# Cross-attention for eight batches on one core: other signs in the seven-product form, and product 6 of y in blocks

## The chip, the core and the metric

One core of one Trainium2 chip. It has a matrix engine (TensorE, PE in the profile), three engines for elementwise work (VectorE, DVE; ScalarE, ACT; GpSimd, POOL), a queue engine that issues transfers (SyncE, SP), an on-chip memory, accumulation banks that PE writes (PSUM) and 16 DMA engines. Each engine runs its own list of instructions in the order in which it was written. The metric is the device time of one execution in microseconds, median of three runs.

## The reference

For each of 8 batches, with x1 and x2 of 512 x 1024 (channels c, positions n or m):

```
q = einsum('bcn,dc->bnd', x1, Wq) + bq          # d = 64
k = einsum('bcn,dc->bdn', x2, Wk) + bk
v = einsum('bcn,dc->bdn', x2, Wv) + bv
attn = softmax(einsum('bnd,bdm->bnm', q, k), axis=2)
out = einsum('bcm,bnm->bcn', v, attn) + x1
```

All of it is float32.

## The kernel before

**The arithmetic.** Per batch the kernel computes scores (m on partitions, n along the free axis), e = exp(score - max), then y = x2 times e, and out = Wv times (y / sum of e) + bv + x1. Both products, of y (stage "y") and of out (stage "o"), use the seven-product form of a 2 x 2 block multiplication. The left operand of y is x2 transposed in blocks a11 .. a22 with sums S1 .. S4, the right one is e in blocks t11 .. t22 (t11 and t21 for the first half of n, t12 and t22 for the second) with sums T1 .. T4. The products are numbered 1 to 7. Product 6 is S2 times T2, and its result is wanted together with product 1.

**Product in one piece or in blocks.** A product in one piece (`multiply`, L420) is 8 calls of the matrix multiply with 512 columns, which the trace shows as 16 instructions. A product in blocks (`multiply_seeded`, L595) is the same seven-product form once more inside: seven small products of two calls each with 256 columns, 28 instructions in the trace. For that DVE first makes inner sums of the left operand (`left_stream`, L478, four instructions) and of the right operand (`right_stream`, L491, three), and afterwards adds one small product to the result (`complete`, L626). ACT copies five partial results while PE works. Before, products 5, 7, 3 and 4 of y are done in blocks in all batches, 1 and 2 in batches 2 to 8, and product 6 in one piece (`first(6)`), added in PSUM on top of product 1.

**The order.** The order of every engine's work is written out by hand in `period` (L868), one call per batch; in the text "batch 1" is the one with s.b = 0. In the steady state PE runs, for batch s and the next batch n: y products 1, 2, 6; scores of n's first half and n's queries; y products 5, 7, 3; scores of n's second half and n's keys; y product 4; then o products 1, 6, 2, then 5, 7 and 3 mixed (`multiply_57`, L545), then o product 4, and batch n's product 1. `multiply_57` leaves o product 7 in bank c; DVE completes it (L591), reads it out with product 5's copy (`evict_o(s, "22")`, L716), and o product 4 (`second(4)`, L437 with output ps_oc) then accumulates on top in the same bank.

**The softmax.** The maximum over m of half h is taken by DVE over the tiles (`fold`, L248, L258) and by POOL across partitions (`highest`, L264); then DVE subtracts it tile by tile (`lower`, L299) and ACT takes the exponential (L308). The sum over m of the first half is made by transfers that add: ACT copies tile 0 (L729) and POOL issues three adding DMAs one after another (`add_tile`, L724), each adding to the same tile, so that each is issued when the one before has landed. The sum of the second half is made by DVE with three folds (L248, output "sum"). Both are then reduced across partitions by POOL (`total`, L269), sent to a column (`few`, L271), inverted by DVE (L277), sent to DRAM (`row`, L279) and spread back (L284).

**Sums made by transfers.** A DMA issued by POOL can add to its destination. S1 (from a block that SP loads), S2, S3, T3 and T4 (from a copy or a negated copy by ACT) are made in that way; S4 is a DVE instruction in batches 2 to 8 (L108). The results 11, 22 and 12 of out get x1 added in this way too (L720) before SP sends them out (L721).

In `period`, the place of the first half's third adding DMA and the second half's maximum:

```
        if five:
            weave(folds(n, 1, "max", ALU.max))
        complete_4 = multiply_seeded(s, 4, "r", hooks, "c" if n else "a")
        if five:
            highest(n, 1)
        complete_4()
        ...
        evict_y(s, "21")
        if five:
            add_tile(n, 0, 3)
            add_11(n, "S3")
        scale_y(s, "21")
```

## Time and profile before

| what | value |
|---|---|
| median of three runs (lowest, highest) | 678.31 us (677.18, 678.32) |
| the profiled execution: its time, its span | 677.15 us, 675.4 us |
| busy time of PE, DVE, ACT, POOL | 666.4, 612.5, 358.5, 218.2 us |
| moved by DMA | 134.26 MB, mean 199 GB/s |
| mean granted clock of PE | 0.998 |

A row of a timeline gives the start in microseconds, the duration, the engine, the line of the kernel, the operation, output and inputs, shapes and a count; in brackets stands idle time of the engine ahead of it and what ended that. Rows of one engine can overlap a little, because the duration runs to the write of the last result; the distance between two starts is what one instruction costs its engine. A matmul's end is modelled, so that PE too is read by distances between starts, and "the chain of waits in order of time" gives these as lengths. A window row gives each engine's busy time in a stretch with the number of instructions, the granted clock (PEclk), and the share of the DMA engines that was busy. The time of an execution is its span and 1.75 us around it (677.15 - 675.4).

### The profile page before, as it was taken

What the parts mean: (1) busy time and instruction counts of PE and PEld (TensorE: products, weight loads), DVE (VectorE), ACT (ScalarE), POOL (GpSimd) and SP (SyncE); (2) the same over time, 40 slices, a digit from 0 to 9 for tenths busy, and PEclk for the clock granted to TensorE, in tenths of its full rate; (3) what the DMA queues carried; (4) which work ended last, traced back from release to release, by engine and by line L of the source; (5) the groups of instructions that cost most, each with busy time, mean ns of one, the idle gap of its engine ahead of it and who ended that gap; (6) DMA issues with size and microseconds to landing.
All of it is one profiled execution on the core that took longest, in us unless ns stands there. A gap on an engine that the chain in (4) does not pass through costs nothing.

```text
span 675.4 us, 7565 instructions
## 1 busy us (share of the span) xinstructions
PE 666.4 (99%) x2510; PEld 413.1 (61%) x2510; DVE 612.5 (91%) x811; ACT 358.5 (53%) x619; POOL 218.2 (32%) x188
## 2 busy tenths in 40 slices
PE   8999999999999999999999999999999999999996
PEld 5334754766556665657656486574855757566853
DVE  1999999999999889998999979999899989999984
ACT  3755456366465464654745647445565456565321
POOL 0126206260344411642134411445122460153400
PEclk9999999999999999999999999999999999999999
DMA  9678798958997959969599695996969968489412
GB/s 304 272 207 278 190 264 152 247 116 245 249 212 192 196 172 301 173 184 249 152 276 190 179 267 151 240 214 175 270 108 222 218 136 231 94 154 251 80 42 98
DMA packets 51638, 134.26 MB, mean 199 GB/s; under 512 B 5648, under 2 KB 7952, under 8 KB 51600
## 3 DMA queue, kind: packets, MB, share of 16 engines
q0 software_dynamic: 23328, 57.75, 47.9%
q1 hardware_dynamic: 27984, 75.64, 31.0%
q10 hardware_dynamic: 288, 0.39, 0.2%
q8 instruction: 20, 0.33, 0.2%
q14 instruction: 18, 0.15, 0.1%
HBM read 88.35 MB, written 16.81 MB: 156 GB/s over the span
## 4 chain that ended last, share of the span: by engine, by line
PE 87%; DVE 7%; DMA 3%; POOL 1%; issue 1%; SPq 1%; ACT 0%; DVEq 0%; POOLq 0%
PE ps_yc L518 10%; PE ps_ya L437 7%; PE ps_oa L559 6%; PE ps_ya L518 5%; PE ps_oa L437 5%; PE ps_s L228 5%; PE ps_o L437 4%; PE ps_oc L437 4%; PE ps_o L457 4%; PE ps_q L181 4%; PE ps_k L181 3%; PE ps_i4chain L518 3%; PE ps_i5chain L518 3%; PE ps_i7chain L518 3%; PE ps_i3chain L518 3%; PE ps_i1chain L518 2%
## 5 line engine op out<-in xcount | busy, mean ns | idle before, releaser
L269 POOL PARTITION_ALL_REDUCE den<-sum x16 | 52.5, 3283 | 72.7 <-DVE few L277 52.6
L724 POOL DMA_DIRECT2D sum<-e x21 | 27.9, 1328 | 145.7 <-ACT sum L729 71.6
L299 DVE TENSOR_TENSOR e<-e,top 128x1024 f32<-128x1024 f32 x60 | 70.6, 1218 | 0.4 <-POOL top L264 0.4
L308 ACT ACTIVATE e<-e 128x1024 f32<-128x1024 f32 x60 | 61.5, 1055 | 8.4 <-DVE e L299 7.8
L237 ACT COPY e<-ps_s 128x1024 f32<-128x1024 f32 x46 | 45.7, 1031 | 8.3 <-PE ps_s L228 8.3
L437 PE MATMUL ps_ya<-eT,aS 128*128 128x512 f32 x112 | 49.5, 593 | 0.0
L228 PE MATMUL ps_s<-q,k 64*128 64x512 f32 x188 | 47.5, 609 | 0.8 <-ACT q L751 0.8
L264 POOL PARTITION_ALL_REDUCE top<-max x16 | 31.0, 1940 | 52.1 <-DVE few L277 20.4
L248 DVE TENSOR_TENSOR max<-max,e 128x1024 f32<-128x1024 f32 x30 | 36.7, 1225 | 2.5
L437 PEld LDWEIGHTS ps_ya<-eT,aS 128*128 128x128 f32 x112 | 21.2, 190 | 24.1 <-issue 23.5
L284 POOL DMA_DIRECT2D den<-row x16 | 9.0, 561 | 78.0 <-DMA row<-few 75.0
L228 PEld LDWEIGHTS ps_s<-q,k 64*128 64x128 f32 x188 | 16.8, 186 | 24.8 <-issue 16.3
L720 POOL DMA_DIRECT2D r<-in_x_dram x14 | 29.3, 2090 | 2.9 <-ACT r L711 2.9
L648 DVE TENSOR_TENSOR y<-y,den 128x1024 f32<-128x1024 f32 x24 | 29.3, 1220 | 0.2
L437 PE MATMUL ps_o<-y,w 128*128 128x512 f32 x64 | 28.8, 592 | 0.0
L457 PE MATMUL ps_o<-y,w 128*128 128x512 f32 x64 | 28.8, 592 | 0.0
L437 PE MATMUL ps_oa<-yT,w_S 128*128 128x512 f32 x64 | 28.8, 592 | 0.0
L437 PE MATMUL ps_oc<-yT,w 128*128 128x512 f32 x64 | 28.8, 592 | 0.0
L611 ACT COPY ps_yc<-ps_i7chain 128x256 f32<-128x256 f32 x32 | 11.4, 357 | 30.3 <-PE ps_i7chain L518 22.3
L611 ACT COPY ps_ya<-ps_i5chain 128x256 f32<-128x256 f32 x32 | 11.4, 358 | 29.9 <-PE ps_i5chain L518 25.7
L485 DVE TENSOR_TENSOR aI<-a,aI 128x256 f32<-128x256 f32 x60 | 26.0, 433 | 1.0
L611 ACT COPY ps_ya<-ps_i1chain 128x256 f32<-128x256 f32 x28 | 10.0, 357 | 30.6 <-PE ps_i1chain L518 27.0
(257 smaller groups left out, 1734.8 us busy)
## 6 DMA issues: line engine op xcount, KB each, us to landing
x_in_x_dram<-in_x_dram SPq DMA_DIRECT2D x60, 512.0 KB, 9.3
a<-in_x2T_dram SPq DMA_DIRECT2D x32, 512.0 KB, 9.5
sum<-e POOLq DMA_DIRECT2D x21, 512.0 KB, 7.5
eT<-eT POOLq DMA_DIRECT2D x16, 512.0 KB, 10.9
aS<-in_x2T_dram POOLq DMA_DIRECT2D x15, 512.0 KB, 7.4
uo<-in_x_dram POOLq DMA_DIRECT2D x14, 512.0 KB, 9.6
r<-in_x_dram POOLq DMA_DIRECT2D x14, 512.0 KB, 11.5
out_dram<-r SPq DMA_DIRECT2D x14, 512.0 KB, 3.4
```

The lines of the kernel that those rows point to most:

```text
L181: nc.tensor.matmul(ps[r, :], w_sb[:, c, :], s.x[:, c, ts(h, H)], start=(c == 0), stop=(c == CT - 1),)
L228: nc.tensor.matmul(ps[g], s.k[r, ts(i, P)], s.q[r, ts(h, H)], start=True, stop=True)
L237: nc.scalar.copy(e[:, :, i, :], whole)
L248: nc.vector.tensor_tensor(f, e[:, :, 0, :] if i == 1 else f, e[:, :, i, :], op)
L269: nc.gpsimd.partition_all_reduce(s.den[h], s.mx[h][:, 0, :], P, ReduceOp.add)
L299: nc.vector.tensor_tensor(e, e, top, ALU.subtract)
L308: nc.scalar.activation(e, e, AF.Exp)
L437: nc.tensor.matmul(ps[:, n], left[ka][:, k, ts(j, P)], right[kb][:, k, n], start=opens and k == 0, stop=i in (2, 3, 4) and k == n_k - 1, s ...
L457: nc.tensor.matmul(ps, w["11"][:, k, ts(j, P)], s.y["11"][:, k, :], start=k == 0, stop=False, skip_group_check=True)
L518: nc.tensor.matmul(ps, s.inner[i][ka][:, k, :], s.inner[i, "t"][kb][:, k, :], start=opens and k == 0, stop=z in (2, 3, 4) and k == n_k - 1 ...
L559: nc.tensor.matmul(ps[:, n], w[ka][:, k, ts(j, P)], s.y[kb][:, k, n], start=False, stop=i == 3 and k == 1, skip_group_check=True,)
L611: nc.scalar.copy(out, of)
```

## The change

**Signs.** At the outer level of y, S1 becomes a21 - a22, S2 a11 - S1, S4 a12 - S2; T2 becomes T1 + t22, T3 t22 + t12, T4 T2 - t21. S1 and S4 start from a negated copy by ACT, T4 too, and T3 needs no negation any more (ACT's two instructions at L341 go). S1's first half, which SP loaded, is now that copy, and POOL adds the other block.

**T3 as a sum.** T3 = t12 + t22 is a sum of e's second half over pairs of tiles, so the softmax's sum of that half takes one fold of T3 (`sum_1`) in place of three. It waits for the DMA that makes T3.

**Product 6 in blocks** in batches 2 to 6 (`six`): inner sums by DVE ahead of it, seven small products, the result copied out by ACT (`copy_u6`) and product 1 added to it by a DMA of POOL; its completion comes later on DVE.

**S4** in batches 2 to 6: a negated copy by ACT and an adding DMA of POOL, in place of DVE's instruction.

**Moves.** The adding DMA and the output of result 12 (`leave`) move into the next period, behind T3's DMAs; S2 of the next batch is made earlier (`early_s2`); the reduction of the second half's sum and T4's DMAs come after the scores; the reciprocal of the first half's sum comes ahead of product 6's inner sums; the folds of the second half's maximum are spread among the work behind product 4, and `highest(n, 1)` comes behind `add_tile(n, 0, 3)` and `add_11(n, "S3")`. In batch 1 `add_tile(n, 0, 3)` moves forward. In batches 7 and 8 product 6 stays in one piece and the sums for product 5 are made earlier.

The diff, its smaller sign changes and buffer names left out:

```diff
                 nc.vector.tensor_tensor(a["21"], a["11"], a["21"], ALU.subtract)
                 a["S3"] = a["21"]
             elif k == "S4":
-                nc.vector.tensor_tensor(a[k], a["12"], a["S2"], ALU.add)
+                nc.vector.tensor_tensor(a[k], a["12"], a["S2"], ALU.subtract)
             else:
-                x, y, op = {"S1": ("21", "22", ALU.add), "S2": ("11", "S1", ALU.subtract)}[k]
-                nc.vector.tensor_tensor(a[k], a[x], a[y], op)
+                x, y = {"S1": ("21", "22"), "S2": ("11", "S1")}[k]
+                nc.vector.tensor_tensor(a[k], a[x], a[y], ALU.subtract)
...
+            self.six = 1 <= b < B - 2
...
+    def copied_s4(s):
+
+        s.a["S4"] = sb.tile([P, MH, C // 2], F32, tag="aS4", name=f"aS4_{s.b}")
+        nc.scalar.mul(s.a["S4"], s.a["S2"], -1.0)
+
+    def add_s4(s):
+
+        nc.gpsimd.dma_start(s.a["S4"], x2T[s.b, 0, 1], accum_op=ALU.add)
+
     def begin_s1(s):
 
         s.a["S1"] = sb.tile([P, MH, C // 2], F32, tag="aS1", name=f"aS1_{s.b}")
-        nc.sync.dma_start(s.a["S1"], x2T[s.b, 1, 0])
+        nc.scalar.mul(s.a["S1"], s.a["22"], -1.0)
 
     def end_s1(s):
 
-        nc.gpsimd.dma_start(s.a["S1"], x2T[s.b, 1, 1], accum_op=ALU.add)
+        nc.gpsimd.dma_start(s.a["S1"], x2T[s.b, 1, 0], accum_op=ALU.add)
...
     def total(s, h):
         fold_halves(s, h, ALU.add)
+        reduce_total(s, h)
+
+    def sum_1(s):
+
+        t = s.t["T3"]
+        s.mx[1] = sb.tile([P, 2, H], F32, tag="fold", name=f"sum_{s.b}_1", bufs=2)
+        nc.vector.tensor_tensor(s.mx[1], t[:, 0:2, :], t[:, 2:4, :], ALU.add)
+        fold_halves(s, 1, ALU.add)
+
+    def total_1(s):
+        sum_1(s)
+        reduce_total(s, 1)
+
+    def reduce_total(s, h):
...
     def right_sums(t, k):
 
-        x, y = {"T1": ("12", "11"), "T2": ("T1", "22"), "T3": ("22", "12"), "T4": ("21", "T2")}[k]
-        nc.vector.tensor_tensor(t[k], t[x], t[y], ALU.add if k == "T4" else ALU.subtract)
+        x, y = {"T1": ("12", "11"), "T2": ("T1", "22"), "T3": ("22", "12")}[k]
+        nc.vector.tensor_tensor(t[k], t[x], t[y], ALU.subtract if k == "T1" else ALU.add)
...
-    def copy_t4(s):
-
-        s.t["T4"] = t4 = sb.tile([P, MH, H], F32, tag="eT4", name=f"eT4_{s.b}")
-        for i in (0, 2):
-            nc.scalar.copy(t4[:, i : i + 2, :], s.t["21"][:, i : i + 2, :])
+    def copy_t4(s, parts=(0, 2)):
+
+        if parts[0] == 0:
+            s.t["T4"] = sb.tile([P, MH, H], F32, tag="eT4", name=f"eT4_{s.b}")
+        t4 = s.t["T4"]
+        for i in parts:
+            nc.scalar.mul(t4[:, i : i + 2, :], s.t["21"][:, i : i + 2, :], -1.0)
...
     def sum_t3(s, i):
 
         t3 = s.t["T3"][:, i : i + 2, :]
-        nc.scalar.mul(t3, t3, -1.0)
         nc.gpsimd.dma_start(t3, s.t["22"][:, i : i + 2, :], accum_op=ALU.add)
+
+    def copy_u6(s, j):
+        if j == 0:
+            s.tmp[6] = sb.tile([P, 2, H], F32, tag="u6", name=f"uy6_{s.b}")
+        nc.scalar.copy(s.tmp[6][:, j, :], s.bank["a", j])
 
     def copy_u1(s, j):
         if j == 0:
-            s.tmp[1] = sb.tile([P, 2, H], F32, tag="yT1", name=f"uy1_{s.b}")
+            s.tmp[1] = sb.tile([P, 2, H], F32, tag="y22" if s.six else "yT1", name=f"uy1_{s.b}")
         nc.scalar.copy(s.tmp[1][:, j, :], s.bank["a", j])
...
-        nc.scalar.copy(s.tmp[7][:, j, :], s.bank["c", j])
+        nc.scalar.mul(s.tmp[7][:, j, :], s.bank["c", j], -1.0)
...
-    def evict_o(s, k):
+    def evict_o(s, k, hook=None):
...
+            if hook:
+                hook()
...
-        if k != "21":
-            nc.gpsimd.dma_start(o, block(s, k, x1), accum_op=ALU.add)
-        nc.sync.dma_start(block(s, k, out), o)
+        def leave():
+            if k != "21":
+                nc.gpsimd.dma_start(o, block(s, k, x1), accum_op=ALU.add)
+            nc.sync.dma_start(block(s, k, out), o)
+
+        if k == "12":
+            return leave
+        leave()
...
-            if s.b:
+            if s.six:
+                copy_u6(s, 0)
+                copy_u6(s, 1)
+                nc.gpsimd.dma_start(s.tmp[6], s.tmp[1], accum_op=ALU.add)
+                reduce_total(s, 1)
+                add_t4(s)
+                weave(folds(n, 0, "max", ALU.max), right_stream(s, 7, s.t["T3"], "yT1", "yT2"))
+                highest(n, 0)
+            elif s.b:
                 for i in range(1, MH):
                     fold(n, 0, i, "max", ALU.max)
                 highest(n, 0)
...
+        def early_s2():
+            negate(n, "S2")
+            add_11(n, "S2")
...
-            s.a["S4"] = sb.tile([P, MH, C // 2], F32, tag="aS4", name=f"aS4_{s.b}")
-            nc.scalar.copy(s.a["S4"], s.a["S2"])
-            nc.gpsimd.dma_start(s.a["S4"], x2T[s.b, 0, 1], accum_op=ALU.add)
+            copied_s4(s)
+            add_s4(s)
...
-            for i in range(1, MH):
-                fold(s, 1, i, "sum", ALU.add)
-            total(s, 1)
             sum_e(s, "T3")
+            total_1(s)
...
-            complete_1 = multiply_seeded(s, 1, "y11")
+            complete_1 = multiply_seeded(s, 1, "y11", {6: lambda: copied_s4(s)} if s.six else {})
+            if s.b == 1:
+                complete_1()
             sum_e(s, "T1", "T2")
-            complete_1()
-            sums_5 = left_stream(s, 5, s.a["S1"], "i2"), right_stream(s, 5, s.t["T1"], "y21", "u1")
-            if n:
-                weave(folds(s, 1, "sum", ALU.add), left_stream(s, 7, s.a["S3"], "yT4"))
-                total(s, 1)
-                invert(s, 0)
-            else:
-                weave(folds(s, 1, "sum", ALU.add), left_stream(s, 7, s.a["S3"], "yT4"))
-                weave(*sums_5)
-            complete_2 = multiply_seeded(
-                s, 2, "y22", {5: lambda: copy_u1(s, 0), 4: lambda: copy_u1(s, 1)}
+            if s.b > 1:
+                complete_1()
+            sums_5 = (
+                left_stream(s, 5, s.a["S1"], "i2"),
+                right_stream(s, 5, s.t["T1"], "u5" if s.six else "y21", "u1"),
             )
             sum_t3(s, 0)
             sum_t3(s, 2)
+            s.leave()
+            if n:
+                invert(s, 0)
+            if s.six:
+                add_s4(s)
+                weave(left_stream(s, 6, s.a["S2"], "i2"), right_stream(s, 6, s.t["T2"], "yT2", "y21"))
+            else:
+                weave(*sums_5)
             if n is None:
-                total(s, 1)
+                weave(left_stream(s, 7, s.a["S3"], "yT4"))
+            complete_2 = multiply_seeded(
+                s, 2, "yT1" if s.six else "y22", {5: lambda: copy_u1(s, 0), 4: lambda: copy_u1(s, 1)}
+            )
             complete_2()
             evict_y(s, "11")
-            copy_t4(s)
-            add_t4(s)
-            first(6, (0,) if n and nn is None else range(2))
+            if s.six:
+                complete_6 = multiply_seeded(
+                    s, 6, "top", {6: lambda: copy_t4(s, (0,)), 4: lambda: copy_t4(s, (2,))}
+                )
+            else:
+                copy_t4(s)
+                add_t4(s)
+                first(6, (0,) if n and nn is None else range(2))
             if n:
+                weave(left_stream(s, 7, s.a["S3"], "yT4"))
+            if s.six:
+                sum_1(s)
                 weave(*sums_5)
+            else:
+                sum_a(s, "S4")
+                if n:
+                    total_1(s)
             if n:
-                sum_a(s, "S4")
                 evict_q = scores_0()
                 spread(s, 0)
-                shares(s, 1)
-            if n:
+                if not s.six:
+                    shares(s, 1)
+            if s.six:
+                pass
+            elif n:
                 weave(right_stream(s, 7, s.t["T3"], "yT1", "yT2"), left_stream(s, 3, s.a["S4"], "aI3"))
             else:
-                sum_a(s, "S4")
                 weave(right_stream(s, 7, s.t["T3"], "yT1", "yT2"), left_stream(s, 3, s.a["S4"], "aI3"))
+                total_1(s)
                 invert(s, 0)
                 spread(s, 0)
             complete_5 = multiply_seeded(
                 s, 5, "r", {6: evict_q} if five else {}, "a"
             )
             complete_5()
-            if n is None:
+            if s.six:
                 shares(s, 1)
-            if n:
+                weave(right_stream(s, 3, s.t["22"], "eT1"), left_stream(s, 3, s.a["S4"], "aI3"))
+                lower(n, 0, 0)
+            elif n:
                 weave(right_stream(s, 3, s.t["22"], "eT1"), lowers(n, 0, 0, 1))
             else:
                 inner_right(s, 3, s.t["22"], "eT1")
...
             copy_7(s, 0)
             if n:
                 lower(n, 0, 1)
+            if s.six:
+                complete_6(s.tmp[6][:, 1, :])
             complete_3 = multiply_seeded(s, 3, "r", hooks, "c")
             if n is None:
                 inner_left(s, 4, s.a["22"], "a12")
+                shares(s, 1)
             join_67(s)
             evict_y(s, "22")
             if n is None:
...
         if n:
             if s.b:
                 load_a(n, "11")
-            begin_s1(n)
             if nn is None:
                 load_x(n, x1)
             if nn:
...
                 exponential(n, 0, 0)
             elif nn:
                 first_sum()
+            begin_s1(n)
             end_s1(n)
             if nn:
                 next_keys()
...
         if s.b == 0:
             sum_y(s, "T1")
         if five:
-            weave(folds(n, 1, "max", ALU.max))
+            fold(n, 1, 1, "max", ALU.max)
         hooks = {}
         if s.b == 0:
             hooks = {6: lambda: exponential(n, 0, 1), 4: lambda: copy_first(n, 0)}
...
             if nn is None:
                 hooks[7] = first_sum
         complete_4 = multiply_seeded(s, 4, "r", hooks, "c" if n else "a")
-        if five:
-            highest(n, 1)
         complete_4()
         if late and n:
             negate(n, "S3")
...
         if five:
             add_tile(n, 0, 3)
             add_11(n, "S3")
+        if five:
+            fold(n, 1, 2, "max", ALU.max)
         scale_y(s, "21")
+        if five:
+            fold(n, 1, 3, "max", ALU.max)
         if s.b == 0:
             add_tile(n, 0, 1)
             sum_y(s, "T4")
         if late and n:
             sum_y(s, "T1")
         if five:
+            highest(n, 1)
             weave(iter_t4(s), right_stream(s, "o7", s.y["T3"], "eT1"))
         elif s.b:
             sum_y(s, "T4")
...
             value_sums("S3", "S4")
             inner_w["o7"] = left_values("21")
         second(6)
+        if s.b == 0:
+            add_tile(n, 0, 3)
         if n:
             add_x1(s, "21")
         if s.b == 0:
...
             lower(n, 1, 0)
             lower(n, 1, 1)
         second(2)
-        evict_o(s, "11")
+        evict_o(s, "11", early_s2 if nn else None)
         if n:
-            if not five:
+            if not nn:
                 add_tile(n, 0, 3)
             if late:
                 inner_left(n, 1, n.a["11"], "i2")
...
             complete_7()
         else:
             second(7)
-        if n:
+        if n and not nn:
             negate(n, "S2")
             add_11(n, "S2")
         evict_o(s, "22")
...
             inner_left(n, 1, n.a["11"], "i2")
         if n:
             weave(
-                right_stream(n, 1, n.e[0][:, 0], "yT1", "yT2"), left_stream(n, 2, n.a["12"], "aS4")
+                right_stream(n, 1, n.e[0][:, 0], "yT1", "yT2"),
+                left_stream(n, 2, n.a["12"], "aI3" if n.six else "aS4"),
             )
             inner_right(n, 2, n.e[0][:, 1], "eT4")
             if s.b == 0:
                 second(3)
-            evict_o(s, "12")
+            n.leave = evict_o(s, "12")
             second(4)
             total(n, 0)
             evict_o(s, "21")
```

14 lines of the change are left out of this document (10 added, 4 removed).

## The prediction

> **What bounds the kernel now.** I read the page's busy times first, then the chain of waits, then the timelines of PE, POOL and DVE over one steady period.
>
> ```profile
> span 675.4 us, 7565 instructions
> PE 666.4 (99%) x2510; PEld 413.1 (61%) x2510; DVE 612.5 (91%) x811; ACT 358.5 (53%) x619; POOL 218.2 (32%) x188
> PE 87%; DVE 7%; DMA 3%; POOL 1%; issue 1%; SPq 1%; ACT 0%; DVEq 0%; POOLq 0%
> 300.42:382.00 81.58, 81.58 (x312) 51.51 (x312) 75.50 (x101) 45.67 (x79) 28.23 (x24) 1.00 0.85 210
> 545.20:626.80 81.60, 80.94 (x300) 54.13 (x297) 78.19 (x106) 44.05 (x81) 29.90 (x26) 1.00 0.78 174
> ```
>
> The fourth row is one steady period as a window: PE has no gap in 81.58 us at clock 1.00, DVE is idle for 6.1 us, ACT for 36 us, and the DMA engines are busy for 0.85 of it. The last row (batch 7) has the only gap of a middle period, 0.66 us. So the kernel ends when PE's list ends: less PE work shortens it one for one, until another engine makes PE wait. PE waits for the last value that it needs, so everything below is about slack: how long before PE needs a value it is there.
>
> **What the change takes from PE.** The first of these rows is from the chain in order of time, the others from PE's timeline.
>
> ```profile
> 375.13 6.87 PE ps_ya L437 x16
> 362.88 1.03 PE L518 MATMUL ps_i1chain<-e,a 128*128 128x256 f32 x4
> 368.93 1.03 PE L518 MATMUL ps_i2chain<-e,a 128*128 128x256 f32 x4
> 374.97 7.03 PE L437 MATMUL ps_ya<-eT,aS 128*128 128x512 f32 x16
> 359.45 3.60 PE L437 MATMUL ps_oc<-yT,w 128*128 128x512 f32 x8
> ```
>
> Product 6 in one piece takes 6.87 us. A product in blocks takes 374.97 - 368.93 = 6.04 us (product 2), and product 1 the same. The gain is 0.83 us in each of five batches: **-4.15 us**. If nothing else moved, this would be the answer, some 674.2 us from the median of 678.31.
>
> **What it adds to DVE.** Costs by groups of instructions; starts follow each other some 0.08 us closer than the durations.
>
> ```profile
> L248 DVE TENSOR_TENSOR sum<-sum,e 128x1024 f32<-128x1024 f32 x18 | 21.9, 1214 | 0.2
> L108 DVE TENSOR_TENSOR aS<-a,aS 128x1024 f32<-128x1024 f32 x7 | 9.0, 1282 | 0.0
> L485 DVE TENSOR_TENSOR aI<-a,aI 128x256 f32<-128x256 f32 x60 | 26.0, 433 | 1.0
> L500 DVE TENSOR_TENSOR eI5y<-eT 128x1024 f32<-128x1024 f32 x8 | 9.7, 1213 | 0.0
> L505 DVE TENSOR_TENSOR eI5u<-eI5y,eT 128x512 f32<-128x512 f32 x8 | 5.4, 680 | 0.0
> ```
>
> Away go two of three folds (2 x 1.21) and S4 (1.28): 3.7 us. Product 6 brings four left sums (4 x 0.43), three right ones (1.21 + 2 x 0.68) and a completion of the same size as the latter (0.68): 5.0 us. The net of +1.3 us fits into the 6.1 us of idle time. So DVE does not become the bound by its sum; what counts is where it has to wait.
>
> **The step that decides: the second half's maximum moves behind a waiting DMA.** POOL's timeline, from batch 4's period (the batches count from 1), with two rows of batch 5's:
>
> ```profile
> 340.19 1.19 POOL L724 DMA_DIRECT2D sum<-e  x1 [5.86 <-ACT ps_yc L611]
> 342.03 1.78 POOL L264 PARTITION_ALL_REDUCE top<-max  x1 [0.64 <-DVE max L258]
> 351.20 1.22 POOL L724 DMA_DIRECT2D sum<-e  x1 [7.38 <-ACT r L711]
> 351.93 1.41 POOL L171 DMA_DIRECT2D a<-in_x2T_dram  x1
> 423.14 1.19 POOL L724 DMA_DIRECT2D sum<-e  x1 [7.22 <-issue]
> 423.89 2.21 POOL L264 PARTITION_ALL_REDUCE top<-max  x1
> L724 POOLq EVENT_SEMAPHORE  x13: 17/7056/9971, 94.9 to 575.7; - x13
> ```
>
> The third adding DMA of a batch's first half stands at 351.20, with 7.38 us of idle POOL ahead of it. The bracket names an ACT instruction that had long ended; the last row shows POOL's own queue standing at this line, with a median of 7.06 us and up to 9.97. What it waits for is the landing of the second adding DMA, issued at 340.19. Before the change the maximum's reduction ran ahead of this wait (342.03). After it, the reduction stands behind it, and behind the DMA for S3 (351.93). Behind S3's issue a reduction starts 0.75 us later and takes 2.21 us when nothing separates them (423.14, 423.89): the maximum is there 0.73 + 0.75 + 2.21 = 3.7 us after the third adding DMA's start.
>
> DVE's timeline shows who waits for it; the first rows are from batch 4's period, the last two from batch 7's, where nothing stands between the subtractions and the read-out.
>
> ```profile
> 350.28 4.62 DVE L299 TENSOR_TENSOR e<-e,top 128x1024 f32<-128x1024 f32 x4
> 357.08 1.41 DVE L716 SCALAR_TENSOR_TENSOR uo<-ps_oc,bv_sb,uo 128x512 f32<-128x512 f32 x2 [0.20 <-PE ps_oc L518]
> 372.22 0.69 DVE L626 TENSOR_TENSOR ps_ya<-ps_ya,v 128x512 f32<-128x512 f32 x1
> 592.51 4.63 DVE L299 TENSOR_TENSOR e<-e,top 128x1024 f32<-128x1024 f32 x4
> 597.66 1.40 DVE L716 SCALAR_TENSOR_TENSOR uo<-ps_oc,bv_sb,uo 128x512 f32<-128x512 f32 x2
>   PEld ps_oc L437: 0.3, 1
> ```
>
> Queued behind the four subtractions of the maximum are the completion of o product 7 and the read-out of bank c (L716); o product 4 on PE (359.45 above) adds into that bank and has to wait for its first half. The last row, from the list of who waited for L716, shows PE doing so once already, for 0.3 us. From the subtractions' start to the read-out's is 597.66 - 592.51 = 5.15 us; its first half takes 0.74 (half of 1.41 and the overlap). With 0.1 us for the start of the subtractions and 0.06 for PE's, both estimates from gaps of that size in these lists, o product 4 can start 3.7 + 0.1 + 5.15 + 0.74 + 0.06 = 9.75 us after the third adding DMA. Here are that DMA and o product 4 in batches 2, 3, 5 and, DMA alone, 6:
>
> ```profile
> 187.82 1.23 POOL L724 DMA_DIRECT2D sum<-e  x1 [7.17 <-ACT r L711]
> 196.29 3.60 PE L437 MATMUL ps_oc<-yT,w 128*128 128x512 f32 x8
> 270.38 1.23 POOL L724 DMA_DIRECT2D sum<-e  x1 [8.15 <-issue]
> 277.87 3.60 PE L437 MATMUL ps_oc<-yT,w 128*128 128x512 f32 x8
> 434.03 1.22 POOL L724 DMA_DIRECT2D sum<-e  x1 [7.93 <-ACT ps_oc L527]
> 441.03 3.60 PE L437 MATMUL ps_oc<-yT,w 128*128 128x512 f32 x8
> 507.71 1.22 POOL L724 DMA_DIRECT2D sum<-e  x1 [0.74 <-issue]
> ```
>
> The distances are 8.47, 7.49, 8.25 (batch 4) and 7.00 us where 9.75 are wanted: PE waits 1.28, 2.26, 1.50 and 2.75 us, together **+7.8 us**. In batch 6 the DMA is 15 us ahead of o product 4 (a period after 441.03), so nothing is lost. All PE work from the copy that begins this chain to o product 4 is unchanged, so the distance carries over.
>
> **What is late next: product 6's inner sums.** DVE now reads bank c just ahead of o product 4 and not 2.37 us ahead (359.45 - 357.08), and keeps the lag. Count from the read-out's start R. By the rows above, the first product's completion ends at R + 15.74 (372.22 + 0.60 - 357.08). After 0.1 us for the reciprocal come S3's sum, the first right sum (both ready at R + 17.45 with the write's end) and S2's (R + 18.7). On PE o product 4 starts at R + 0.80, product 1 3.43 us later, product 6 12.09 after that (374.97 - 362.88), and its second and third small product 0.86 and 1.73 behind its start: R + 17.18 and R + 18.05. PE waits 0.3 and then 0.4 us, in the four batches behind a late maximum: **+2.7 us**. In batch 2 DVE has no such lag: 0, at most one such stall.
>
> **The rest, taken at nothing or little.** Two rows, product 5's start on PE (product 6 ended at 300.42, the first window's start) and POOL's reduction of a sum:
>
> ```profile
> 307.57 1.13 PE L518 MATMUL ps_i5chain<-eT,aS 128*128 128x256 f32 x4
> L269 POOL PARTITION_ALL_REDUCE den<-sum x16 | 52.5, 3283 | 72.7 <-DVE few L277 52.6
> ```
>
> POOL issues two more DMAs a batch (1.2 us each, by L724's rows) in 53 us of idle time; SP loses a load and sends result 12 after 21, with nothing urgent behind. Behind the new wait for product 6's copy, some 6 us after product 6's end (the scores' copies go first), POOL has that DMA, the reduction, T4's two DMAs and the first half's maximum: 1.2 + 3.3 + 2.4 + 2.2 = 9.1 us, so the maximum is there some 15 us after product 6's end. DVE wants it behind product 5's completion (7.15 + 6.04 us) and product 3's sums (3.7 us), at 17 us: 0, and should it be late, the 2 us are the first to go. ACT gets S4's and S1's copies and five partial results and loses T3's negation; its 36 us of idle time hide them, and the copies hang on hooks behind small products. T3's DMA no longer waits for ACT or the second reduction, so `sum_1` finds it landed. T4's DMAs come some 9 us later and are wanted at product 4's sums, behind products 5, 7 and 3 (18 us of PE); the second reciprocal moves likewise, wanted at the scaling after that. If that cover went, PE would wait at product 4. Deferred `leave` and earlier S2 take transfers from ahead of the small column DMA. In batches 7 and 8 DVE loses two folds; batch 7's gap of 0.66 us is the most that this can give: **-0.7 us**. Batch 1's edits: 0, PE does not wait there.
>
> **Sum.** -4.15 + 7.8 + 2.7 - 0.7 = +5.65 us. Against the profiled execution, 677.15 us (1.16 below the median), that is 682.8; against the median 684.0. I take **684.0 us**.
>
> **DMA: a row and a rule.** A window of the stretch between the first and the third adding DMA of batch 4, the issue of the small column (first half's sum), and the landing times of all such columns.
>
> ```profile
> 333.00:351.00 18.00, 18.00 (x58) 10.63 (x57) 17.59 (x22) 9.01 (x15) 4.31 (x4) 1.00 1.00 275
> 369.11 0.60 POOL L271 DMA_DIRECT2D few<-den  x1 [0.30 <-POOL den L269]
> DMA to landing us min/median/max: 1.7/3.5/13.2
> ```
>
> From 333 to 351 the DMA engines are busy for all of the time, which makes the second adding DMA slow; the change takes nothing out of this stretch. The Trainium skill, "DMA: Bandwidth & Descriptors", section "Issuing engines are not separate DMA queues", says that transfers started by any engine run on the same 16 DMA engines and interleave. By that rule the two adding DMAs that the change adds per batch could only push the third one later, never earlier; each microsecond of it would cost four, one in each of batches 2 to 5. The trace agrees with the rule in the row of 1.00.
>
> **Rivals.** (A) The other side, faster: the second adding DMA lands at least 2.75 us earlier, so all four waits at o product 4 vanish and the lag with them. Then 678.31 - 4.15 - 0.7 = 673.5. For it speaks batch 6, where the third DMA comes 15 us ahead of its product; against it the full window above, in which all loads stay. (B) The reciprocal, now ahead of product 6's inner sums, waits for the small column: the DMA at 369.11 starts 12.0 us after R, and a landing of 1.7 to 7 us puts it at R + 13.7 to R + 19, against the reciprocal's place at R + 15.74. Up to 3.3 us more in five batches: at most 16.5, so up to 700; half of that gives 692. For it speaks the maximum of 13.2 among landings; against it that result 12's DMA no longer runs ahead of it. (C) Late maximum but no lag at product 6: 684.0 - 2.7 = 681.3, in the same range. (D) The shared DMA engines push the third adding DMA 1 us later: 688.
>
> **How the numbers follow.** Main case with C, from 680 to 687: 0.60. A, 673 to 677: 0.20. B and D, 687 to 700: 0.16. Gain and loss cancelling: 0.04. The range 673.5 to 690 holds the first, most of A, the last and part of the third, some 0.83; the main case's own is 680 to 687. A change within 0.2% (1.4 us) is about what cannot be told from none. Faster by more: 0.20; same: 0.04; slower: 0.76.
>
> **What would show it.** In the profile after: product 6 as 28 instructions in 6.04 us; POOL's reduction of the second half's maximum right behind S3's DMA; DVE idle some 5 us ahead of the four subtractions, released by POOL; PE's wait of 1 to 3 us at ps_oc L437, released by DVE L716, in batches 2 to 5 and not in 6; short waits at product 6's second and third small product. I am wrong if the third adding DMA starts 10 us or more ahead of o product 4.

## The result: 710.8 us, 34 us slower

The changed kernel takes 710.82 us (median of six runs, 709.54 to 714.42), the kernel before, on the same chip, 677.24 us (median of six, 676.90 to 678.32). The ratio is 1.050, with a 95% interval of 1.0474 to 1.0524. The forecast was 684.0 us and at most 690: slower is right, the size is not.

These are the lines of the page of the changed kernel that answer to those shown of before: the span, the busy times, the shares of the chain of waits by engine, and two groups of instructions (busy us, mean ns of one, then the idle time just before them and what ended it).

```profile
span 710.3 us, 7753 instructions
PE 676.0 (95%) x2570; PEld 429.2 (60%) x2570; DVE 609.0 (86%) x830; ACT 367.3 (52%) x642; POOL 246.4 (35%) x198
PE 28%; DVE 8%; POOL 4%; issue 4%; DMA 2%; ACT 2%; DVEq 0%; POOLq 0%
L293 POOL PARTITION_ALL_REDUCE den<-sum x16 | 71.8, 4488 | 56.8 <-DVE sum L268 46.6
L301 DVE RECIPROCAL few<-few 128x4 f32<-128x4 f32 x16 | 2.7, 171 | 31.8 <-DMA few<-den 31.8
```

and batch 5's period as a window (clock third from the end):

```profile
387.77:475.77 88.00, 83.65 (x323) 54.72 (x322) 74.85 (x107) 47.88 (x84) 34.12 (x26) 0.98 0.83 200
```

PE is busy for 95% of the span where it was 99%, VectorE for 86% where it was 91%: no engine became the bound, they wait for each other. The chain adds up to 48% of the span only and is not read further. The period is 88.00 us for 81.58, with 4.35 us of gaps and a clock of 0.98. Two groups have changed. POOL's reduction of a sum takes 4488 ns on average where it took 3283, and the reciprocals of VectorE are preceded by 31.8 us of idle time. The list of what PE waited for (us in total, times, the longest) names the places.

```profile
PE ps_oc L467 <- DVE uo L754: 9.2, 4, 3.5
PE ps_i3third L548 <- DVE aI L515: 5.9, 4, 2.1
PE ps_ya L548 <- ACT ps_ya L644: 3.5, 1, 3.5
PE ps_i3chain L548 <- DVE aI L515: 3.1, 4, 0.8
PE ps_i3chain L548 <- ACT ps_yc L644: 2.9, 3, 1.2
PE ps_i7third L548 <- DVE eI7yT L530: 1.1, 1, 1.1
```

To see where the span of 675.4 us grew by 34.9, I took from PE's timeline the start of each product in each batch, in both kernels, and subtracted the lengths of the stages between them (a stage reaches to the next product's start; stages that differ by less than 0.2 us in all batches are left out):

```
us after - before     batch 2    3      4      5      6
products 1 and 2        +6.65   0.00   0.00   0.00   0.00
product 6               -0.82  -0.13  -0.83  -0.14  -0.14
product 3               +0.86  +4.93  +3.74  +4.40  +3.96
o products              +2.80  +5.50  +1.55  +2.15   0.00
```

Product 3 lost 17.9 us, the o products 12.0, batch 2's products 1 and 2 6.7, and product 6 gained 2.1: 34.5 together. Batch 1 adds 0.8 and batch 7 0.8, batch 8 takes off 1.1 (its last stage counted to the end of the span), and the stages left out 0.1, which makes up the 34.9.

**The o products.** The timeline of POOL, VectorE and PE at the end of batch 4's period (in brackets the idle time ahead of an instruction and what ended it):

```profile
374.38 1.19 POOL L767 DMA_DIRECT2D sum<-e  x1 [9.65 <-ACT r L747]
375.70 2.55 POOL L274 PARTITION_ALL_REDUCE top<-max  x1
378.29 4.63 DVE L323 TENSOR_TENSOR e<-e,top 128x1024 f32<-128x1024 f32 x4 [3.93 <-POOL top L274]
383.44 1.40 DVE L754 SCALAR_TENSOR_TENSOR uo<-ps_oc,bv_sb,uo 128x512 f32<-128x512 f32 x2
384.23 3.70 PE L467 MATMUL ps_oc<-yT,w 128*128 128x512 f32 x8 [1.28 <-DVE uo L754]
296.51 5.40 PE L467 MATMUL ps_oc<-yT,w 128*128 128x512 f32 x8 [3.54 <-DVE uo L754]
```

This is the forecast chain: the third adding DMA, the reduction behind it, the subtractions, the read-out, o product 4, which starts 9.85 us after the DMA (forecast 9.75). The last row is batch 3's, with the longest of these waits; the product behind it takes 5.40 us instead of 3.70.

**Product 3.** The same view, later in batch 5:

```profile
413.03 0.85 POOL L944 DMA_DIRECT2D uy<-uy  x1 [11.76 <-ACT uy L372]
413.60 7.76 POOL L293 PARTITION_ALL_REDUCE den<-sum  x1
421.66 0.58 POOL L295 DMA_DIRECT2D few<-den  x1 [0.30 <-POOL den L293]
407.55 0.69 DVE L268 TENSOR_TENSOR sum<-sum 128x512 f32<-128x512 f32 x1
417.58 0.68 DVE L268 TENSOR_TENSOR max<-max 128x512 f32<-128x512 f32 x1
426.83 0.18 DVE L301 RECIPROCAL few<-few 128x4 f32<-128x4 f32 x1 [6.36 <-DMA few<-den]
426.93 1.19 DVE L530 TENSOR_TENSOR eI3eT<-e 128x1024 f32<-128x1024 f32 x1
428.60 1.10 PE L548 MATMUL ps_i3third<-eI3eT,aI 128*128 128x256 f32 x4 [1.48 <-DVE aI L515]
430.48 2.05 PE L548 MATMUL ps_i3chain<-eI3eT,aI 128*128 128x256 f32 x4 [0.77 <-DVE aI L515]
```

The sum is ready at 408.24, but its reduction stands behind product 6's DMA, which waits for ACT's copy, until 413.60. It then takes 7.76 us, the small column is back some 5 us after that, and VectorE's reciprocal waits for the column for 6.36 us. Behind the reciprocal, in VectorE's order, stand the inner sums of product 3. Nothing needs the reciprocal's value yet; what is late is what is queued behind it.

**Batch 2, product 1.** ACT's and PE's timeline:

```profile
126.27 1.06 ACT L156 ACTIVATE aS<-aS 128x1024 f32<-128x1024 f32 x1 [4.27 <-DMA aS<-in_x2T_dram]
127.65 2.08 PE L548 MATMUL ps_ya<-e,aI 128*128 128x256 f32 x4 [3.51 <-ACT ps_ya L644]
```

S4's copy is an instruction of ACT placed between the small products of product 1 (a hook). It waits for S2's adding DMA, and ACT's copies of product 1's partial results stand behind it. The product loses 4.7 us and product 2, at a lower clock, 2.0. In the profiles of four runs below that leave this place alone PE waits 3.2 to 3.3 us, product 2 keeps its length, and the loss is 3.5 to 3.6.

**The clock.** The stages lost more than PE waited. Windows of PE's granted clock (eighth column, after the five engines' busy times): across the first wait of product 3 in batch 3, behind its second one, and at o product 4 of batches 3 and 4.

```profile
250.00:252.90 2.90, 1.10 (x4) 0.68 (x4) 2.90 (x6) 0.37 (x1) 0.56 (x1) 1.00 1.06 210
253.20:255.20 2.00, 1.99 (x5) 1.64 (x6) 2.00 (x4) 0.00 (x0) 0.00 (x0) 0.50 0.32 116
296.50:300.30 3.80, 3.79 (x6) 1.63 (x7) 3.80 (x7) 0.94 (x2) 1.20 (x1) 0.61 1.05 184
384.20:387.90 3.70, 3.67 (x9) 1.76 (x10) 3.70 (x7) 0.96 (x2) 1.20 (x1) 1.00 1.05 187
```

Behind the longer waits the clock falls to 0.50 and 0.61; behind the wait of 1.28 us it stays at 1.00.

### The profile page after: what moved, and what is told of

The parts are those of the page before. It is cut to its first block, busy times and chain, and to the rows that moved or that the text cites. A ratio compares the mean times of both kernels' runs of the same rounds, so it can differ in the third digit from the quotient of the medians.

```text
span 710.3 us, 7753 instructions
## 1 busy us (share of the span) xinstructions
PE 676.0 (95%) x2570; PEld 429.2 (60%) x2570; DVE 609.0 (86%) x830; ACT 367.3 (52%) x642; POOL 246.4 (35%) x198
## 5 line engine op out<-in xcount | busy, mean ns | idle before, releaser
L293 POOL PARTITION_ALL_REDUCE den<-sum x16 | 71.8, 4488 | 56.8 <-DVE sum L268 46.6
L323 DVE TENSOR_TENSOR e<-e,top 128x1024 f32<-128x1024 f32 x60 | 70.6, 1218 | 20.6 <-POOL top L274 20.5
L274 POOL PARTITION_ALL_REDUCE top<-max x16 | 39.0, 2434 | 29.1 <-DVE max L872 18.8
L258 DVE TENSOR_TENSOR max<-max,e 128x1024 f32<-128x1024 f32 x30 | 40.5, 1350 | 0.4
L467 PE MATMUL ps_oc<-yT,w 128*128 128x512 f32 x64 | 30.9, 628 | 9.2 <-DVE uo L754 9.2
L301 DVE RECIPROCAL few<-few 128x4 f32<-128x4 f32 x16 | 2.7, 171 | 31.8 <-DMA few<-den 31.8
L681 DVE TENSOR_TENSOR y<-y,den 128x1024 f32<-128x1024 f32 x24 | 29.2, 1219 | 0.1
L467 PEld LDWEIGHTS ps_oc<-yT,w 128*128 128x128 f32 x64 | 12.4, 199 | 27.0 <-issue 13.8
L644 ACT COPY ps_ya<-ps_i1chain 128x256 f32<-128x256 f32 x28 | 9.9, 356 | 34.5 <-PE ps_i1chain L548 31.4
L759 POOL DMA_DIRECT2D r<-in_x_dram x14 | 27.2, 1944 | 0.0
L944 POOL DMA_DIRECT2D uy<-uy x5 | 4.3, 854 | 63.0 <-ACT uy L372 63.0
```

The lines of the kernel that those rows point to most:

```text
L258: nc.vector.tensor_tensor(f, e[:, :, 0, :] if i == 1 else f, e[:, :, i, :], op)
L274: nc.gpsimd.partition_all_reduce(s.top[h], s.mx[h][:, 0, :], P, ReduceOp.max)
L293: nc.gpsimd.partition_all_reduce(s.den[h], s.mx[h][:, 0, :], P, ReduceOp.add)
L323: nc.vector.tensor_tensor(e, e, top, ALU.subtract)
L467: nc.tensor.matmul(ps[:, n], left[ka][:, k, ts(j, P)], right[kb][:, k, n], start=opens and k == 0, stop=i in (2, 3, 4) and k == n_k - 1, s ...
L681: nc.vector.tensor_tensor(s.y[k], s.y[k], rden, ALU.mult)
```

## The experiments

My theory after the result: three separate waits of an engine that holds other work behind it (POOL at the third adding DMA, VectorE at the second reciprocal, ACT at S4's copy), each made dearer by the clock. The rivals are with each run. Unless another is named, an edit is to the changed kernel. All times are medians against the kernel before on the same chip (677.3 to 677.7).

### The maximum's reduction first

```diff
-        if five:
-            add_tile(n, 0, 3)
-            add_11(n, "S3")
...
             highest(n, 1)
+            add_tile(n, 0, 3)
+            add_11(n, "S3")
```

> The changed kernel with one move: in batches 2 to 6 POOL issues the reduction of the second half's maximum ahead of the third adding DMA and S3's DMA, as the kernel before had it; VectorE's order stays. Theory 1 (POOL's order makes o product 4 wait): the four waits of PE at ps_oc L467 for VectorE's read-out (together 9.2 us, with the lower clock behind them about 12 us) vanish, the time falls from 710.8 to about 699, and the stalls at product 3 stay. Theory 2 (VectorE is late by its own load, or the maximum's folds come late, whatever POOL does): the waits at o product 4 stay for the most part and the time stays above 706.

Measured: 701.65 us, ratio 1.0362 (1.0345 to 1.038). The waits at o product 4 are gone from the list, and product 6 gains 0.82 to 0.83 us in all five batches: the lag of the inner sums went with them. Product 3 stays, with 21.6 us by stages, 3.7 more than in the changed kernel, which takes back a part of the gain: the time is 2.7 us above the expected 699. Theory 1 holds.

### The second reciprocal behind product 3's sums

```diff
             if s.six:
-                shares(s, 1)
                 weave(right_stream(s, 3, s.t["22"], "eT1"), left_stream(s, 3, s.a["S4"], "aI3"))
...
                 complete_6(s.tmp[6][:, 1, :])
+                shares(s, 1)
```

> The changed kernel with one move: in batches 2 to 6 VectorE's reciprocal of the second half's sum, and the two DMAs that spread it, come behind the inner sums of product 3 and behind product 6's last addition. Theory 1 (the reciprocal stands ahead of product 3's inner sums and waits for its small column): PE's waits at product 3 (5 batches, with the lower clock about 18 us in all) vanish and the time falls from 710.8 to about 693; POOL's reduction still takes 7 to 8 us where it stands beside additions of two operands in SBUF. Theory 2 (VectorE's own work ahead of product 3 is too long for the 18 us): waits at product 3 stay, over 705. Theory 3 (the late reduction also holds up the first half's maximum): the wait only moves from the reciprocal to the first subtraction behind product 3's sums, the time comes to 695 to 705, and the losses appear at products 3 and 4 as before.

Measured: 690.26 us, ratio 1.0203 (1.0168 to 1.0239). Product 3's stages are 0.00 us longer in batches 3 to 6 and 0.21 in batch 2. In this run's timeline POOL's reduction is as slow as before:

```profile
399.18 7.76 POOL L293 PARTITION_ALL_REDUCE den<-sum  x1
```

The time fell by 20.6 us, 2.6 more than expected; by stages product 3 gives 17.7, and 3.0 come from batch 2's products 1 and 2, which this edit doesn't touch. A slow reduction alone costs PE nothing: the place of the instruction that waits for it does. Theory 1 holds, and the late maximum of theory 3 is not seen at PE.

### S4 later in batch 2

```diff
-            complete_1 = multiply_seeded(s, 1, "y11", {6: lambda: copied_s4(s)} if s.six else {})
+            complete_1 = multiply_seeded(s, 1, "y11", {6: lambda: copied_s4(s)} if s.six and s.b > 1 else {})
...
             if s.six:
-                add_s4(s)
+                if s.b > 1:
+                    add_s4(s)
...
             evict_y(s, "11")
+            if s.b == 1:
+                copied_s4(s)
+                add_s4(s)
```

> The changed kernel with one move, in batch 2 alone: ACT's copy of S2 into S4 and the adding DMA of S4 come behind product 2 and not on a hook inside product 1. Theory 1 (in batch 2 this copy waits for S2's adding DMA and, in order, holds up ACT's copy of product 1's first partial result): PE's wait of 3.5 us in product 1 of batch 2 vanishes, and with the lower clock behind it 5 to 6.5 us: about 705. Theory 2 (S2's data are late for PE's own left operands too): PE waits a little later in product 2 instead and the time stays above 709.

Measured: 708.90 us, ratio 1.0462 (1.0447 to 1.0478), where 705 was expected. The wait in product 1 is gone and products 1 and 2 are as long as before. A part of it comes back at product 6, whose right sums are late; the first reciprocal waits ahead of them (timeline of VectorE and PE):

```profile
130.91 0.18 DVE L301 RECIPROCAL few<-few 128x4 f32<-128x4 f32 x1 [0.77 <-DMA few<-den]
132.70 1.10 PE L548 MATMUL ps_i6third<-eI6yT,aI 128*128 128x256 f32 x4 [1.49 <-DVE eI6yT L530]
```

Of the 6.7 us in products 1 and 2, 2.1 return there, and product 3 of batch 2 is late by 4.39 us instead of 0.86: the stall had hidden the next. Neither theory had this.

### The maximum's move alone, in the kernel before

```diff
         if five:
-            highest(n, 1)
+            fold_halves(n, 1, ALU.max)
...
             add_tile(n, 0, 3)
             add_11(n, "S3")
+            highest(n, 1, halves=False)
```

> The kernel before with one move, a part of the change done alone: in batches 2 to 6 POOL's reduction of the second half's maximum comes behind the third adding DMA and S3's DMA; VectorE's order stays. Theory 1 (the prediction's term): PE waits at o product 4 in four batches for 7.8 us, and the lower clock behind these waits adds 1 to 4 us: 685 to 690 against 677.2. Theory 2 (in the changed kernel o product 4 is late for another cause, the later folds on VectorE among them): within 1.5 us of 677.2.

Measured: 689.38 us, ratio 1.0174 (1.0154 to 1.0195). PE's timeline, o product 4 of batches 2 to 5:

```profile
198.26 3.70 PE L437 MATMUL ps_oc<-yT,w 128*128 128x512 f32 x8 [1.23 <-DVE uo L716]
283.52 5.39 PE L437 MATMUL ps_oc<-yT,w 128*128 128x512 f32 x8 [3.42 <-DVE uo L716]
368.48 3.70 PE L437 MATMUL ps_oc<-yT,w 128*128 128x512 f32 x8 [1.42 <-DVE uo L716]
453.01 5.40 PE L437 MATMUL ps_oc<-yT,w 128*128 128x512 f32 x8 [2.69 <-DVE uo L716]
```

The waits were forecast as 1.28, 2.26, 1.50 and 2.75. They are 8.8 us for 7.8, and the two longer ones make the product itself 1.7 us longer (5.40 for 3.70): 12 us. This is the prediction's deciding step, alone and with its price.

### The sum reduced early

```diff
+            if s.six:
+                total_1(s)
             complete_2()
             evict_y(s, "11")
...
             if s.six:
-                sum_1(s)
...
-                reduce_total(s, 1)
```

> The changed kernel with one move: in batches 2 to 6 VectorE's two additions of the second half's sum stand ahead of product 2's completion, and POOL reduces that sum at once, beside VectorE's additions that read PSUM, and not after product 6's copy. The reciprocal stays ahead of product 3's inner sums. Theory 1 (POOL's reduction is held up by VectorE's additions of two operands in SBUF beside it, 7 to 8 us for 3.2): it takes 3.2 to 4.5 us in its new place, the small column is back before the reciprocal, the waits at product 3 vanish, and the time falls from 710.8 to about 692, like with the late reciprocal. Theory 2 (the reduction is slow for other reasons, such as the many transfers under way): it takes 7 to 8 us in the new place too; the reciprocal still has its column early, the time is the same, about 692. Theory 3 (the sum waits for T3's adding DMA when it stands this early): VectorE is late with product 6's inner sums, PE waits there, above 700.

Measured: 699.41 us, ratio 1.0322 (1.0309 to 1.0336). In the new place, beside VectorE's additions that read PSUM, the reduction takes 3.23 us in all five batches, and product 3 is as long as before. But the two additions wait for T3's DMA when they stand this early, VectorE is late with y11, and PE waits for it at the scores' bank c; timeline and list of waits:

```profile
399.24 3.23 POOL L293 PARTITION_ALL_REDUCE den<-sum  x1 [6.02 <-DVE sum L268]
PE ps_sc L238 <- DVE y L695: 4.4, 4, 1.8
```

Theory 1 holds for the reduction. Theory 2's transfers don't explain its length: in this fast stretch (399.0 to 402.5) the DMA engines are busy for 0.95 of the time, in the slow one of the changed kernel (413.6 to 418.2) for 0.86. Theory 3 holds for the wait of the additions, but PE pays at the scores (8.2 us by stages) and not at product 6.

### Both moves

The first two edits together.

> The changed kernel with both moves: the reduction of the second half's maximum ahead of the third adding DMA, and the second reciprocal behind product 3's inner sums. If the two losses are separate, the gains add up: 710.8 - 9.2 - 20.5 = about 681, with no wait of PE at o product 4 or product 3, product 6 at 0.83 us less than before in batches 2 to 6, and what is left is batch 2's wait in product 1 (3.5 us) and similar waits of 1 to 2 us behind S4's copy. If the lag of VectorE merely moves on to the next product, 684 or more.

Measured: 682.11 us, ratio 1.0061 (1.0045 to 1.0078). The two gains add up to within 1.0 us: the losses are separate.

### Both moves, and S4 and the first reciprocal later

```diff
-            complete_1 = multiply_seeded(s, 1, "y11", {6: lambda: copied_s4(s)} if s.six else {})
+            complete_1 = multiply_seeded(s, 1, "y11", {})
...
-            if n:
+            if n and not s.six:
                 invert(s, 0)
             if s.six:
-                add_s4(s)
                 weave(left_stream(s, 6, s.a["S2"], "i2"), right_stream(s, 6, s.t["T2"], "yT2", "y21"))
+                invert(s, 0)
...
             evict_y(s, "11")
             if s.six:
+                copied_s4(s)
+                add_s4(s)
```

> The changed kernel with both moves, and in batches 2 to 6 S4's copy and adding DMA behind product 2 and the first reciprocal behind product 6's inner sums, so that neither ACT inside product 1 nor VectorE ahead of product 6 waits for a transfer. If these are all the places at which the change loses time, what is left is its gain, 0.83 us in each of five batches and nothing else: 677.3 - 4.2 + 0.5 for batch 7 = 673 to 674. If the gain is eaten by some wait that the others covered, 676 or more.

Measured: 677.73 us, ratio 1.0009 (0.999 to 1.0027). The expected 673 to 674 was missed: batches 3, 5 and 6 are 0.82 us shorter each, but batches 2, 4 and 7 are 1.1 to 1.4 us longer. In batch 4 the timeline shows why:

```profile
305.17 1.22 DVE L530 TENSOR_TENSOR eI5u<-eT 128x1024 f32<-128x1024 f32 x1 [3.81 <-DMA out_dram<-uo]
307.16 3.49 POOL L293 PARTITION_ALL_REDUCE den<-sum  x1
307.25 2.69 DVE L515 TENSOR_TENSOR aI<-aS,aI 128x256 f32<-128x256 f32 x1
```

The change writes product 5's right sums into the tile of result 22, and they wait for its store. VectorE is late, meets POOL's reduction just as that starts, and an addition of 0.42 us takes 2.69.

### The same with the early sum

The edit before, with the early sum of the fifth run in place of the late second reciprocal.

> As the run before in its four places, but the second half's sum is added and reduced early, ahead of product 2's completion, and its reciprocal stays ahead of product 3's inner sums: if the early reduction alone removes the wait for the small column, 673 to 675 as well; if the two additions ahead of product 2's completion wait for T3's adding DMA, 677 or more.

Measured: 690.08 us, ratio 1.0179 (1.0154 to 1.0203): the early additions cost 1.5 to 4.7 us a batch at the scores, as in the fifth run.

### Product 6 in one piece

```diff
-            self.six = 1 <= b < B - 2
+            self.six = False
```

> The changed kernel without its change of product 6: in all batches product 6 is computed in one piece and S4 by VectorE, as in the last two; the other signs, the second half's sum from T3, the later result 12 and the later maximum stay. Theory 1 (the stalls at product 3 come from product 6's blocks, whose copy and transfer go ahead of POOL's reduction; the stalls at o product 4 from the maximum's place): PE waits at o product 4 in four batches as in the run with that move alone, and not at product 3: 689 to 692. Theory 2 (the stalls at product 3 come from the sum over T3): they stay, 700 or more.

Measured: 694.76 us, ratio 1.0261 (1.0234 to 1.0288); the profiled run is the fastest of its four (687.83; the others 693.41 to 697.21), and where these lose 6 to 9 us more is not seen. In the profile product 3 is as before in all batches, and o product 4 waits four times, 1.1 to 1.9 us. Theory 1 holds for the places. A wait that nobody expected stands in product 5 of batch 2 (ACT's timeline), 4.42 us by stages:

```profile
149.69 0.37 ACT L644 COPY v<-ps_i5third 128x256 f32<-128x256 f32 x1 [3.91 <-DMA out_dram<-r]
```

That copy writes the tile of result 12, whose store the change has put off.

### Waits of measured length, in the kernel before

```diff
+            for _ in range((0, 8, 10, 12, 14, 16)[s.b]):
+                nc.vector.tensor_tensor(spare, spare, spare, ALU.add)
         evict_o(s, "22")
```

> The kernel before, with idle additions of 128x256 on VectorE ahead of result 22's read-out of bank c in batches 2 to 6, one after another 8, 10, 12, 14 and 16 of them at some 0.33 us each, so that PE waits at o product 4 for about 1, 1.7, 2.4, 3 and 3.7 us; their results are not used. Theory 1 (a wait of PE of more than some 2.6 us lowers its clock and costs 1.7 us more, a shorter one nothing): o product 4 takes 3.7 us in the first three batches and 5.4 us in the last two. Theory 2 (the lower clock belongs to the crowded transfers or to VectorE's load at these places in the changed kernel): 3.7 us in all of them.

Measured: 704.20 us, ratio 1.0388 (1.0362 to 1.0414). The additions took 0.46 us each, so the waits are longer than meant. PE's timeline, o product 4 of batches 2 to 6:

```profile
199.58 3.70 PE L437 MATMUL ps_oc<-yT,w 128*128 128x512 f32 x8 [1.52 <-DVE uo L716]
283.87 3.70 PE L437 MATMUL ps_oc<-yT,w 128*128 128x512 f32 x8 [2.44 <-DVE uo L716]
369.08 6.55 PE L437 MATMUL ps_oc<-yT,w 128*128 128x512 f32 x8 [3.36 <-DVE uo L716]
458.06 6.44 PE L437 MATMUL ps_oc<-yT,w 128*128 128x512 f32 x8 [4.28 <-DVE uo L716]
547.84 5.92 PE L437 MATMUL ps_oc<-yT,w 128*128 128x512 f32 x8 [5.20 <-DVE uo L716]
```

Waits of 1.52 and 2.44 us leave the product at 3.70; longer ones cost 2.2 to 2.9 us on top, with nothing changed but VectorE's additions. Theory 1 holds at this place, where its 1.7 us was too little; that its limit of 2.6 us is not a general one, the last section shows.

### Result 12 at once, batch 7's reciprocal later

The four moves, and:

```diff
-            s.leave()
...
-            n.leave = evict_o(s, "12")
+            evict_o(s, "12")()
...
-                if not s.six:
-                    shares(s, 1)
...
+            if n and not s.six:
+                shares(s, 1)
             complete_7 = multiply_seeded(s, 7, "y12")
```

> As the run with four moves (both moves, S4 and the first reciprocal later), and result 12's adding DMA and its store at once, as the kernel before had them, and in batch 7 the second reciprocal behind product 7's sums. Theory 1 (product 5's right sums wait for the store of result 12, whose tile they write, and batch 7's product 7 waits for the small column): the waits of batches 2, 4 and 7 vanish but for batch 2's at product 6, and the time comes to 674 to 675.5, under the kernel before. Theory 2 (the store's transfers take the way of the small column or of S4): as without these two moves, 677 to 678.

Measured: 680.08 us, ratio 1.0041 (1.0026 to 1.0056). Batch 7 came down from +1.43 to +0.43 us by stages, but product 5 of batch 2 lost 4.37 and product 3 of batches 3 to 5 up to 0.99. Theory 1 was wrong on result 12: with its store at once, product 5's sums still wait for result 22's (0.71 us in batch 4). And theory 2 is borne out in another place: result 12's adding DMA now goes ahead of T3's, and VectorE waits for T3 ahead of the second half's sum, which it did for 1.8 us in all before these two moves. From the list of VectorE's waits:

```profile
DVE sum L284 <- DMA e<-e: 11.1, 5, 4.6
```

The longest, 4.6 us, stands in batch 2 ahead of product 5's sums. So the change's later result 12 (`leave`) is what lets `sum_1` find T3 landed.

### The old tile for product 5's sums

The four moves, batch 7's reciprocal later, and:

```diff
-            if s.b == 1:
-                complete_1()
             sum_e(s, "T1", "T2")
-            if s.b > 1:
-                complete_1()
+            complete_1()
...
-                right_stream(s, 5, s.t["T1"], "u5" if s.six else "y21", "u1"),
+                right_stream(s, 5, s.t["T1"], "y21", "u1"),
```

> As the run with four moves (result 12 later, as in the change), and three more: product 5's right sums go back into the tile that the kernel before used for them, so that VectorE does not wait there for the store of result 22; in batch 2 product 1's completion goes back behind T1 and T2; in batch 7 the second reciprocal comes behind product 7's sums. If the waits that were left in batches 2, 4 and 7 come from these places, they vanish (together some 3.5 us of stages longer than before), and the time comes to 674 to 675: the change's gain of 0.83 us in five batches, and faster than both kernels. If VectorE or a transfer is late at the next place instead (T3's adding DMA ahead of the sum in batch 2), 676.5 to 678.

Measured: 674.11 us (673.55 to 674.59), ratio 0.9949 (0.9935 to 0.9963): 0.5% faster than the kernel before. Page, and the window of batch 4's period:

```profile
span 672.8 us, 7756 instructions
PE 663.1 (99%) x2570; PEld 424.6 (63%) x2570; DVE 622.2 (92%) x830; ACT 365.2 (54%) x642; POOL 256.3 (38%) x198
281.75:362.50 80.75, 80.75 (x323) 53.78 (x322) 77.48 (x106) 47.33 (x84) 34.43 (x26) 1.00 0.94 225
```

A steady period is 80.75 us without a gap, 0.83 less than 81.58. Left over are a wait of 1.3 us for S4's copy at product 6 of batch 2, which makes that product 1.15 us longer than before, and one of 0.2 us at product 3 of batch 5. The spans differ by 2.6 us: product 6 gives 2.15 over the five batches, batch 8 1.07, and the rest loses 0.65.

## Why the prediction was wrong in size

The span grew by 34.9 us where 5.65 were forecast. Of the 29.2 us between, 17.9 are product 3's, 6.7 those of products 1 and 2 in batch 2, and 4.2 the o products', which lost 12.0 for 7.8. The first two stood in the forecast at nothing.

- **"What the change takes from PE", -4.15 us: right.** Product 6's stage is 0.82 to 0.83 us shorter wherever VectorE is in time. The text's "If nothing else moved, this would be the answer, some 674.2 us" is near what the last run measured, 674.11, but in part by luck: product 6 gives only 2.15 us there and batch 8 another 1.07, which the forecast did not have, and the forecast started from a median of 678.31 where the kernel before measured 677.71 beside that run.
- **"The step that decides", +7.8 us: right in place and cause, too small in price.** o product 4 started 9.85 to 9.87 us behind the third adding DMA at all four forecast places, for 9.75, and batch 6 did not wait. The waits were 8.8 us alone and 9.2 in the changed kernel (2.53, 3.54, 1.28 and 1.88 for the forecast 1.28, 2.26, 1.50 and 2.75), so that their sum is closer than its parts. The missing term is the clock: alone, two of the waits, 2.69 and 3.42 us, cost 1.7 us more each.
- **"Late next", +2.7 us: right.** Product 6 kept 0.69 to 0.70 of its 0.83 us from being gained in batches 3, 5 and 6, 2.1 us in all. In batch 4, behind the longest wait of PE and a slower o product 4, the lag was gone.
- **"the second reciprocal moves likewise", at 0 us: the step that failed.** I asked who wants the reciprocal's value, found 18 us of PE ahead of it, and did not ask what VectorE has queued behind the reciprocal. These are product 3's inner sums: 17.9 us by stages, taken away whole by moving that instruction (0.00 in batches 3 to 6). The size of the delay was wrong too: the reduction, counted at 3.3 us, took 7.76 beside VectorE's additions. The forecast 15 us from product 6's end to the maximum is 19.1 in batch 5 (406.68 to 425.79).
- **"the copies hang on hooks behind small products", at 0 us: failed in batch 2.** 36 us of idle time of ACT hide nothing when one copy waits for a transfer: 6.7 us in this profile, of which 3.5 are the wait and the rest mostly PE's lower clock; 3.5 to 3.6 us in the four others.
- **"In batches 7 and 8", -0.7 us: -0.3 came.** Batch 8 gained 1.1, and batch 7 lost 0.8: a reciprocal that waits 3.01 us stands ahead of product 7's sums again.
- **"`sum_1` finds it landed": right** at its place (VectorE did not wait for it there), and wrong one product earlier, as the early sum showed, or with result 12's transfers ahead of T3's.
- **Rival B** was the right mechanism at the wrong reciprocal: the first one waited in batch 2 by 0.77 us, once S4 was out of the way, and in batch 4 by 0.3 to 0.7 us in several runs, where product 6 lost nothing. A did not happen: all four waits were there, in the changed kernel as with the move alone. D (third adding DMA later) fits a part: in the changed kernel the waits of batches 2 and 3 were 1.3 us longer than forecast, with the move alone only batch 3's was, by 1.2, and batch 5's wait in the changed kernel was 0.9 shorter. Why the distances shift so stays open.

## What to carry to other kernels

When an instruction that waits for a transfer is moved, look first at what its engine has queued behind it, and only then at who needs its result: here an instruction whose value had 18 us to spare cost PE 17.9 us over five batches, and moving one line took all of it away. Price a wait of the matmul engine with the clock that it costs, and the duration of an instruction with what will run beside it. When a stall is removed, expect the next one to show (S4, product 5's tile, batch 7): the gain of 3.6 us came only with edits at all seven places.

## What the hardware showed that I had not expected

**POOL's reduction and VectorE exclude each other.** The reduction takes 3.23 us beside reads of PSUM and mostly 7.0 to 9.0 us where it starts during a run of VectorE's additions of two operands in SBUF. In batch 5 of the changed kernel that run ended at 418.26 and the reduction at 421.36, 3.1 us later, about its own length: as if it ran only when the run was over. In batch 4 of the run with four moves it came first, and VectorE's addition took 2.69 us. The Trainium skill, "SBUF — State Buffer", section "SBUF: two separate sides", says that VectorE's instructions with two SBUF inputs and GpSimd's share a pair of ports as an exclusive lock: who starts first has it, the other is blocked. The traces agree in that one is blocked, and add that back-to-back additions can keep the reduction out over many instructions, here for some 4.5 us. Who comes first is not plain from the starts: in batch 2 of the run with four moves an addition that starts 0.12 us ahead of the reduction takes 2.89 us.

**A short wait can halve the matmul clock.** At o product 4, single waits of PE up to 2.53 us cost nothing more, those from 2.69 us on made the product 1.5 to 2.9 us longer, with the clock at 0.61 in the window shown. At product 3 two waits of 1.48 and 0.77 us, 1.1 us apart, did the same, and 1.28 and 0.77 did not. Nor is the length of a single wait the rule: the first row is of product 5 in batch 2, with result 12 at once, the second of product 1 in batch 2, with the second reciprocal later (PE's timelines).

```profile
148.39 1.31 PE L548 MATMUL ps_i5third<-eI5u,aI 128*128 128x256 f32 x4 [2.30 <-DVE eI5u L530]
126.78 1.13 PE L548 MATMUL ps_ya<-e,aI 128*128 128x256 f32 x4 [3.33 <-ACT ps_ya L644]
```

Over the 4 us behind the wait of 2.30 us the clock is 0.59, behind that of 3.33 us it is 1.00; three more of 3.2 to 3.3 us at the same place lowered nothing either. The exact rule stays open. The Trainium skill, "TensorE: Matmul & The Clock Gate", section "What's actually happening", has the clock halved after an idle window of about 3.4 us that runs freely; some of the drops here came behind shorter waits, and here the measurement decides.
